# A 7x7 depthwise stage: work moved between ACT, DVE and GpSimd, and taps loaded a call ahead

## The chip, the cores and the metric

The kernel runs on one core of one Trainium2 chip. The metric is the device time of the program in microseconds. Three timed runs and one profiled execution of the kernel before are shown. A core has the engines PE (TensorE, matrix products), DVE (VectorE), ACT (ScalarE), POOL (GpSimd) and SP (which issues transfers). ACT and POOL issue transfers as well. Each engine runs its own instructions in a fixed order and waits on semaphores.

## The reference, cut to what matters

The program has four layers, each of the form x = x + layer(group norm(x)), on x of 4 batches, 384 channels and 64 x 64 pixels in float32. The change concerns the end of the third layer and the fourth.

The third layer ends with a mix that is linear in its second hidden tensor h2: per channel and batch, x2 = wx + gh * h2 + g0. The fourth layer is a depthwise 7 x 7 convolution whose kernel depends on the data:

```
x_w  = gelu(mean(x) @ w_avg.T + b_avg + max(x) @ w_max.T + b_max)
xr   = x_w[:, :, None, None] * w_mix          # 7 x 7 taps of each channel
Gx   = sqrt(sum(xr * xr));  Nx = Gx / (mean over channels of Gx + 1e-6)
kern = gamma * (xr * Nx) + beta
out  = depthwise_conv(x, kern, padding 3);    x = x + out
```

The kernel is therefore a factor of the channel and batch times the fixed taps `w_mix`, plus the constant `beta`. The program computes the two terms apart: a convolution with fixed taps, scaled afterwards, and a plain 7 x 7 box sum, scaled by beta.

## The kernel before, in words

The 384 channels lie in three tiles of 128 channels, j = 0, 1, 2. The stage is `phase_g`. In it:

- **x2.** `x2_of(j, b)` makes x2 for one tile and batch, 128 channels by 4096 pixels, in four quarters of 1024. A tile of wx is loaded into one of three `x` buffers, a quarter of h2 into one of three buffers with the tag `w7` (L1899, SP's queue). ACT scales two halves of it into PSUM (`x_m`, L1903), DVE adds them to x (L1906), ACT squares the sum for the variance (L1908, writing into the h buffer, which thereby becomes free after it), DVE takes the maximum (L1909). After four quarters POOL's queue stores x2 in DRAM (L1911).
- **Opening.** For j = 0 the four batches are made first, and `to_strips` lays each of them out for the convolution: POOL fills the edges (L1922, L1924), ACT scales (`ax`, L1925), PE transposes (L1935), ACT and DVE copy out of PSUM into `z` (L1942, L1940).
- **The fixed taps.** `conv7(j, c0)` convolves 8 channels of a tile, 16 calls for each tile, 48 in all. A call loads its taps (`wmix`, two buffers, L1950, SP's queue). Then, for each of four pairs of channels, an elementwise product of taps and a band mask builds a banded matrix (`toep`, four buffers, L1959), on POOL in every third pair and on DVE otherwise. DVE reads the band from PSUM, POOL from SBUF. PE multiplies it with `z` (eight matmuls of a pair, L1972). For j = 0 and 1 ACT copies the result out and stores it in DRAM (`raw`, L1981); for j = 2 DVE adds it to the rest of the output (L1984), which is stored.
- **The box sums.** `boxes(j, b)` takes a tile of x2 in four parts of 16 rows. POOL adds rows (L2021, L2023), DVE finishes the column of seven (L2024 to L2038). Then, for two halves of a part, PE transposes (`ht_m`, L2044), ACT copies out of PSUM (`ht`, L2046), PE multiplies with a band (`box_m`, L2050), and DVE scales and adds to x (L2052). For j = 0 and 1 `in_raw` is loaded and added (L2062). After four parts POOL's queue stores x (L2066, L2068).
- **Strips of later tiles.** `half_strips` loads x2 of the next tile from DRAM (L1858), ACT scales, PE transposes (L1868), ACT and DVE copy.
- **Factors.** After j = 0, `factors` derives the data-dependent scales from the means and maxima of x2; no box sum can be scaled before.

These functions are generators. The loop in `phase_g` takes them by turns: a call of `conv7` for 8 channels, then a piece of the strips, then up to five pieces of x2 (while j = 0) or of boxes (while j = 1 and 2). A scheduler fixes the order on each engine from the emitted program, with its own estimate of durations, so an instruction may stand earlier or later than it is emitted. It is these fixed orders, one for each engine, that run.

```
for n in range(8):
    self.conv7(j, 64 * half + 8 * n)
    next(strips, None)
    for k in range(5):
        if j == 0 and (k < 2 or k == 2 and n % 2):
            next(x2, None)
        if j == 1 or j == 2 and (k or n % 2):
            next(boxes, None)
```

Of the kernel before, what the change touches and what calls it, by code (L numbers as in the profile page):

```python
# [21 lines left out]
F32 = mybir.dt.float32  # L22
AF = mybir.ActivationFunctionType
ALU = mybir.AluOpType
# [4 lines left out]
NJ = 3  # L29
P = 128  # L30
# [251 lines left out]
class _Builder:  # L282
# [1403 lines left out]
    def phase_g(self):  # L1686

        tc, nc = self.tc, self.nc
        with ExitStack() as ctx:
            self.open_psum(ctx, 3)
            cp = ctx.enter_context(tc.tile_pool(name="g_const", bufs=1))
            self.gw_p = ctx.enter_context(tc.tile_pool(name="g_w", bufs=2))
            self.gt_p = ctx.enter_context(tc.tile_pool(name="g_t", bufs=2))
            self.w_gate = []  # L1700
            for j in range(NJ):
                t = cp.tile([P, 2, C], F32, tag=f"w_gate{j}", name="w_gate")
                for i, k in enumerate(("w_avg_t", "w_max_t")):
                    nc.scalar.dma_start(t[:, i], self.ins[k][:, j])
                self.w_gate.append(t)
            self.mean384 = self.const(cp, "mean384")
            self.band7 = self.const(cp, "band7")
            self.cols7 = self.const(cp, "cols7")

            self.band7_p = self.psum.tile([P, 512], F32, tag="band", name="band7_p", bufs=1)[:, 0:W]  # L1710
            nc.vector.tensor_copy(self.band7_p, self.band7)

            sq = self.gt_p.tile([P, 8 * 64], F32, tag="wmix", name="mix_sq")[:, 0 : NJ * 49]
            nc.vector.tensor_mul(sq, self.vec("w_mix"), self.vec("w_mix"))
            sq = sq.rearrange("p (j k) -> p j k", j=NJ)
            self.mix2 = cp.tile([P, NJ], F32, tag="mix2", name="mix2")
            nc.vector.tensor_reduce(self.mix2, sq, AX.X, ALU.add)
            self.ln_exp(nc.scalar.activation(self.mix2, self.mix2, AF.Sqrt))
            for k in ("a_s", "b_s"):
                setattr(self, k, cp.tile([P, NJ, B], F32, tag=k, name=k))  # L1720

            self.s_s, self.s_b = (cp.tile([P, NJ, B], F32, tag=k, name=k) for k in ("s_s", "s_b"))
            self.a_pair = cp.tile([P, NJ, 2, 2, 2], F32, tag="a_pair", name="a_pair")

            self.gm = cp.tile([P, NJ, B], F32, tag="gm", name="gm")
            self.off = cp.tile([P, NJ, B, 3], F32, tag="off", name="off")
            self.x2_var, self.x2_max = (cp.tile([P, NJ, B, 4], F32, tag=k, name=k) for k in ("x2_var", "x2_max"))


            self.z = self.z_[:, 0 : P * 136].rearrange("p (c k b) -> p c k b", k=34, b=B)  # L1730
            nc.gpsimd.memset(self.z_[:, P * 136 :], 0.0)
            nc.gpsimd.memset(self.z[:, :, 0], 0.0)
            self.group_means()
            behind = iter(())
            for b in range(B):
                for x in self.x2_of(0, b):
                    next(behind, None)
                for _ in behind:
                    pass
                behind = self.to_strips(0, b, x)  # L1740
            for _ in behind:
                pass
            self.pair_scales(1)

            def others(*pieces):
                for p in pieces:
                    yield from p

            x2 = others(*(self.x2_of(j, b) for j in (1, 2) for b in range(B)))
            boxes = others(*(self.boxes(j, b) for j, b in ((2, 0), (2, 1), (2, 2), (2, 3), (0, 0), (0, 1), (0, 2), (0, 3))))
            boxes1 = others(*(self.boxes(1, b) for b in range(B)))
            for j in range(NJ):
                for half in range(2):
                    strips = self.half_strips(j + half, 1 - half) if 0 < j + half < NJ else iter(())
                    for n in range(8):
                        self.conv7(j, 64 * half + 8 * n)
                        next(strips, None)
                        for k in range(5):  # L1760
                            if j == 0 and (k < 2 or k == 2 and n % 2):
                                next(x2, None)
                            if j == 1 or j == 2 and (k or n % 2):
                                next(boxes, None)
                    for _ in strips:
                        pass
                if j == 0:
                    for _ in x2:
                        pass
                    self.factors()  # L1770
                    self.pair_scales(2)
                if j == 1:
                    boxes = others(boxes, boxes1)
            for _ in boxes:
                pass
# [110 lines left out]
    def x2_of(self, j, b):  # L1886

        nc = self.nc
        at = lambda v: v[:, j, b : b + 1]
        if self.x2_ahead:  # L1890
            x = self.x2_ahead.pop(0)
        else:
            x = self.gx_tile("x2")
            nc.sync.dma_start(x, self.wx[b][:, j])
        for q in range(4):
            sl = slice(q * 1024, (q + 1) * 1024)

            h = self.gw_p.tile([P, 1024], F32, tag="w7", name="g_h2", bufs=3)
            nc.sync.dma_start(h, self.h2[b][:, j, sl])  # L1899
            for v in range(2):  # L1900
                m = self.pm("x2_m")
                part = slice(q * 1024 + v * 512, q * 1024 + v * 512 + 512)
                nc.scalar.activation(  # L1903
                    m, h[:, v * 512 : v * 512 + 512], AF.Identity, bias=at(self.g0), scale=at(self.gh)
                )
                nc.vector.tensor_add(x[:, part], x[:, part], m)  # L1906

            nc.scalar.activation(h, x[:, sl], AF.Square, bias=at(self.neg2), accum_out=self.x2_var[:, j, b, q : q + 1])  # L1908
            nc.vector.tensor_reduce(self.x2_max[:, j, b, q : q + 1], x[:, sl], AX.X, ALU.max)  # L1909
            yield None  # L1910
        nc.gpsimd.dma_start(self.scratch["x2"][b][j], x)  # L1911
        yield x

    def to_strips(self, j, b, x):
# [3 lines left out]
        for part in range(3):  # L1918
# [23 lines left out]
                    nc.scalar.copy(zv, mv.rearrange("p k c -> p c k"))  # L1942
            yield

    def conv7(self, j, c0):


        nc = self.nc
        wmix = self.gt_p.tile([P, 8 * 64], F32, tag="wmix", name="wmix")
        nc.sync.dma_start(wmix, self.ins["mix_t"][j][:, c0 : c0 + 8].rearrange("p c t n -> p (c t n)"))  # L1950
        o = self.gt_p.tile([P, 8, P], F32, tag="rest", name="rest_o", bufs=3)
        if j == NJ - 1:
            nc.sync.dma_start(o, self.rest[c0 : c0 + 8].rearrange("c y b n -> (y b) c n"))
        m = self.psum.tile([P, 1024], F32, tag="c", name="conv_m", bufs=2)
        for pair in range(4):
            t = self.gt_p.tile([P, 16, 8, 8], F32, tag="toep", name="toep", bufs=4)
            on_pool = (c0 // 2 + pair) % 3 == 2
            eng, band = (nc.gpsimd, self.band7) if on_pool else (nc.vector, self.band7_p)
            eng.tensor_tensor(  # L1959
                t,  # L1960
# [7 lines left out]
            for c in range(2):  # L1968
                ch = 2 * pair + c
                for i in range(4):  # L1970
# [5 lines left out]
                        start=i == 0,  # L1976
                        stop=i == 3,
                    )
        of = o.rearrange("p c n -> p (c n)")
        if j < NJ - 1:  # L1980
            nc.scalar.copy(of, m)  # L1981
            nc.scalar.dma_start(self.raw[j][:, c0 : c0 + 8], o)
            return
        nc.vector.tensor_add(of, of, m)  # L1984
        nc.sync.dma_start(self.out[j][:, c0 : c0 + 8], o)

    def boxes(self, j, b):

# [2 lines left out]
        nc = self.nc  # L1991
        x = self.load_x2(j, b)
        off = lambda k: self.off[:, j, b, k - 6 : k - 5]
        scale = self.b_s[:, j, b : b + 1]
        pairs_of = lambda t, r, n: t[:, r * W : (r + 2 * n) * W].rearrange("p (k r w) -> p k r w", r=2, w=W)
        above, last = None, None
        for part in range(4):
# [42 lines left out]
            for q in range(2):  # L2040
# [3 lines left out]
                    nc.tensor.transpose(m[:, k * P : (k + 1) * P], h[:, at : at + P], self.ident)  # L2044
                ht = self.gt_p.tile([P, 512], F32, tag="ht", name="ht")
                nc.scalar.copy(ht, m)  # L2046
                m = self.pm("box_m")
                for k in range(4):
                    sl = slice(k * P, (k + 1) * P)
                    nc.tensor.matmul(m[:, sl], lhsT=ht[:, sl], rhs=self.cols7, start=True, stop=True)  # L2050
                xq = x[:, (2 * part + q) * 512 : (2 * part + q + 1) * 512]
                nc.vector.scalar_tensor_tensor(xq, m, scale, xq, ALU.mult, ALU.add)  # L2052
                if q == 0:
                    yield
            if j < NJ - 1:
                d = self.gt_p.tile([P, 1024], F32, tag="rest", name="in_raw", bufs=3)
                nc.sync.dma_start(
# [5 lines left out]
            if part == 3:  # L2063
# [2 lines left out]
                    nc.gpsimd.dma_start(self.out[j].rearrange("(b m) c n -> b (m c n)", b=B)[b].rearrange("(c n) -> c n", c=P), x)  # L2066
                else:
                    nc.gpsimd.dma_start(self.rest[:, :, b], x.rearrange("p (y n) -> p y n", n=P))  # L2068
            yield


@with_exitstack
# [29 lines left out]
```

## Time and profile before

| | us |
|---|---|
| median of three runs | 4841.11 (4838.23 to 4847.09) |
| the profiled execution | 4841.52 |
| its span | 4839.6 |
| start of the stage `phase_g`, from the span's start | about 4075 |
| first product of `conv7` | 4163.5 |
| first DVE operation of `factors` with x2's variance | 4354.9 |
| last matmul | 4834 |

Over the whole span PE is busy 91%, DVE 60%, ACT 41% and POOL 16%; the stage of this document is the last 765 us of it. In that stage the sums are: PE 599, DVE 611, ACT 335 and POOL 315 us.

How to read the lines of the profile that follow: a line of the groups gives the line of the code, the engine, the operation, output and inputs, their shapes and the count, then the busy time in us and the mean of one in ns, and after the next bar how long the engine stood idle just before these instructions, and what ended that idle time. A line of the waits gives who waited, for whom, the total in us, the number of times and the longest. A transfer's profile interval is its issue, not its transfer. Matmul records are two for each float32 matmul in the code and one for each transpose; they overlap, so their durations don't add up to time.

### The profile page before, as it was taken

The numbers are of one execution on the slowest core, as the hardware profiler recorded it, in microseconds if no ns is written. First come the engines' busy times: TensorE is split into PE (matmuls) and PEld (weight loads), VectorE is DVE, ScalarE is ACT, GpSimd is POOL, SyncE is SP. The second block draws the span as 40 slices with busy tenths as digits, with TensorE's granted clock in tenths as the row PEclk, the third lists the DMA queues.
The fourth block names the chain that finished last, engine by engine and source line by source line (L and its number), as shares of the span: only waits on it lengthen the run. The fifth ranks groups of instructions, "written<-read, shape, count | busy, mean of one in ns | idle before, by whom it ended". The sixth has DMA issues, their size and how long they took to land.

```text
span 4839.6 us, 49747 instructions
## 1 busy us (share of the span) xinstructions
PE 4399.5 (91%) x18445; PEld 2453.7 (51%) x18445; DVE 2892.0 (60%) x4647; ACT 1996.9 (41%) x2976; POOL 757.7 (16%) x643
## 2 busy tenths in 40 slices
PE   6999999999999999989987898699999997778888
PEld 2233444344443444435477787344444443678888
DVE  7766556645656455556867777555521113767898
ACT  4444444444444444336345566211133334763321
POOL 1000000000000000000044554000000001235544
PEclk9999999999999999989988999899999998788999
DMA  4312212111211111113168898776664444995776
GB/s 145 102 42 66 72 53 75 64 56 42 70 61 63 40 59 59 53 63 120 65 197 282 278 308 299 273 259 251 238 236 153 156 156 152 325 346 183 231 256 232
DMA packets 289663, 747.65 MB, mean 154 GB/s; under 512 B 22555, under 2 KB 123014, under 8 KB 277382
## 3 DMA queue, kind: packets, MB, share of 16 engines
q1 hardware_dynamic: 226744, 454.62, 29.4%
q0 software_dynamic: 36480, 167.01, 9.2%
q10 hardware_dynamic: 26190, 122.76, 6.4%
q8 instruction: 149, 2.44, 0.2%
q14 instruction: 100, 0.82, 0.1%
HBM read 442.04 MB, written 302.25 MB: 154 GB/s over the span
## 4 chain that ended last, share of the span: by engine, by line
PE 32%; DVE 7%; DMA 6%; ACT 3%; issue 2%; POOL 1%; SPq 0%; ACTq 0%; DVEq 0%; POOLq 0%
PE h_m L1658 10%; PE h_s L1604 10%; PE conv_m L1370 6%; PE conv_m L1972 2%; DMA c_d<-d 2%; DMA wmix<-in_mix_t 1%; DMA g_h<-h 1%; DVE toep L1959 1%; PE box_m L2050 1%; DVE in_x L2052 1%; DMA ax<-x 1%; DVE in_x L2062 1%; DMA unit_x<-x 1%; DVE box L2034 0%; ACT g_h L1908 0%
## 5 line engine op out<-in xcount | busy, mean ns | idle before, releaser
L819 ACT ACTIVATE probs<-sc_s 128x1024 f32<-128x1024 f32 x512 | 496.5, 1019 | 695.0 <-PE av L929 594.8
L929 PE MATMUL av<-probs,vt 128*128 128x512 f32 x1536 | 717.7, 604 | 0.0
L1128 DVE SCALAR_TENSOR_TENSOR acc<-band,vecs,acc 128x512 f32<-128x512 f32 x708 | 496.0, 745 | 44.9 <-POOL band L1089 39.6
L1658 PE MATMUL h_m<-f_h,cm_w_t 128*128 128x512 f32 x1152 | 497.3, 595 | 7.4 <-ACT f_h L1646 7.4
L1370 PE MATMUL conv_m<-toep,z 128*128 128x192 f32 (+1 forms) x2304 | 444.2, 354 | 9.5 <-DVE z L1299 9.4
L929 PEld LDWEIGHTS av<-probs,vt 128*128 128x128 f32 x1536 | 277.6, 192 | 339.6 <-issue 335.9
L1972 PE MATMUL conv_m<-toep,z 128*128 128x128 f32 x3072 | 395.5, 287 | 36.5 <-POOL toep L1959 15.8
L1370 PEld LDWEIGHTS conv_m<-toep,z 128*128 128x128 f32 x2304 | 408.5, 197 | 31.6 <-DVE z L1299 10.1
L1972 PEld LDWEIGHTS conv_m<-toep,z 128*128 128x128 f32 x3072 | 381.1, 203 | 38.4 <-POOL toep L1959 16.2
L1604 PE MATMUL h_s<-e_tok,cm_w_t 128*128 128x512 f32 x768 | 362.9, 595 | 4.2 <-DVE e_tok L1589 4.2
L1658 PEld LDWEIGHTS h_m<-f_h,cm_w_t 128*128 128x128 f32 x1152 | 220.4, 191 | 284.4 <-issue 273.3
L1666 DVE BATCH_NORM_STATS2 h_st<-f_h 128x6 f32<-128x512 f32 x96 | 66.5, 694 | 429.8 <-ACT f_h L1665 429.8
L811 PE MATMUL sc_s<-q,k 32*128 32x512 f32 x2048 | 307.1, 643 | 15.1 <-ACT probs L819 14.9
L1351 POOL TENSOR_TENSOR toep<-w,band 128x1280 f32<-128x1280 f32 x94 | 272.6, 2900 | 237.5 <-PE conv_m L1370 234.3
L1051 PE MATMUL t_m<-w_in_t,xb 128*128 128x384 f32 x768 | 282.0, 503 | 3.4 <-DVE coef L1068 3.2
L965 PE MATMUL proj_m<-xm,w_proj_t 128*128 128x512 f32 x576 | 270.3, 609 | 6.4 <-DVE xm L904 4.9
L1611 ACT COPY e_h<-h_s 128x1024 f32<-128x1024 f32 x96 | 97.2, 1012 | 400.2 <-PE h_s L1604 400.2
L1613 DVE BATCH_NORM_STATS2 h_st<-e_h 128x6 f32<-128x512 f32 x192 | 123.4, 685 | 204.9 <-ACT e_h L1611 204.7
L1604 PEld LDWEIGHTS h_s<-e_tok,cm_w_t 128*128 128x128 f32 x768 | 146.9, 191 | 187.9 <-issue 183.1
L1051 PEld LDWEIGHTS t_m<-w_in_t,xb 128*128 128x128 f32 x768 | 144.4, 194 | 141.6 <-issue 62.5
L972 DVE SCALAR_TENSOR_TENSOR x_res<-proj_m,bn_c,x_res 128x512 f32<-128x512 f32 x96 | 71.7, 747 | 240.2 <-PE proj_m L965 240.2
L1604 PE MATMUL h_s<-z,cm_w_t 128*128 128x512 f32 x384 | 196.7, 594 | 0.0
(423 smaller groups left out, 6396.3 us busy)
## 6 DMA issues: line engine op xcount, KB each, us to landing
d<-d_o ACTq DMA_DIRECT2D x48, 1024.0 KB
c_d<-d SPq DMA_DIRECT2D x48, 1024.0 KB
hid<-e_h ACTq DMA_DIRECT2D x16, 3072.0 KB
f_h<-hid SPq DMA_DIRECT2D x16, 3072.0 KB
x_in<-in_x SPq DMA_DIRECT2D x96, 256.0 KB
x_res<-in_x SPq DMA_DIRECT2D x32, 768.0 KB
xa<-x_res POOLq DMA_DIRECT2D x32, 768.0 KB, 3.9
xa_out<-xa SPq DMA_DIRECT2D x32, 768.0 KB
```

What stands on the lines that cost most here:

```text
L811: nc.tensor.matmul(s[:, g], lhsT=k4[32 * g : 32 * g + 32, c], rhs=q[i][32 * g : 32 * g + 32], start=True, stop=True,)
L819: nc.scalar.activation(p[:, h * 1024 : (h + 1) * 1024], s[:, 2 * h : 2 * h + 2].rearrange("p a b -> p (a b)"), AF.Exp, scale=0.25,)
L929: nc.tensor.matmul(av[0], lhsT=vt[:, 4 * c + v, :], rhs=p[:, v * 512 : (v + 1) * 512], start=c == 0 and v == 0, stop=c == 7 and v == 3,)
L965: nc.tensor.matmul(m, lhsT=self.w_proj[:, j, o * P : (o + 1) * P], rhs=xm[:, j], start=j == 0, stop=j == NJ - 1,)
L1051: nc.tensor.matmul(m[:, 0:C], lhsT=xb[:, j], rhs=self.w_in[:, j, :], start=j == 0, stop=j == NJ - 1,)
L1128: nc.vector.scalar_tensor_tensor(out, src(j, k), w, done, ALU.mult, ALU.add)
L1351: eng.tensor_tensor(t, self.w53[:, at : at + 160].rearrange("p (m n) -> p m n", n=8).unsqueeze(2).to_broadcast([P, 20, 8, 8]), band.rearra ...
L1370: nc.tensor.matmul(m[:, c * 256 + to : c * 256 + to + 64 * (k1 - k0)], lhsT=self.z_[:, at : at + P], rhs=t[:, 10 * c + k0 : 10 * c + k1].r ...
L1604: nc.tensor.matmul(s[:, v, :], lhsT=w1[:, j, o * P : (o + 1) * P], rhs=t[j][:, v * 512 : (v + 1) * 512], start=j == 0, stop=j == NJ - 1,)
L1613: nc.vector.bn_stats(st[:, o, 8 * b + 2 * i + v, :], h[:, o, v * 512 : (v + 1) * 512])
L1658: nc.tensor.matmul(m, lhsT=w2[:, o, j * P : (j + 1) * P], rhs=h[:, o, v * 512 : (v + 1) * 512], start=o == 0, stop=o == 5,)
L1972: nc.tensor.matmul(m[:, ch * P : (ch + 1) * P], lhsT=self.z_[:, at : at + P], rhs=t[:, 8 * c + 2 * i : 8 * c + 2 * i + 2].rearrange("p m a ...
```

## The change

Four edits, all in the last stage:

1. In `x2_of`, for j = 0 alone, the product gh * h2 + g0 runs on POOL over the whole quarter, in place in the h buffer, and one DVE add of 1024 columns takes it from SBUF. For j = 1 and 2 ACT and PSUM are used as before.
2. The taps are loaded by a new function `load_mix`, on POOL's queue, at the start of the call before the one that uses them; the first is loaded ahead of the loop.
3. `conv7` becomes a generator that yields after each pair and at its end, so that the pieces of x2 or boxes come between pairs. For j = 1 and 2 every second pair's product is on POOL, for j = 0 every third as before.
4. In `boxes`, the matmul with the band and the add that follows move into `box_sums` and are emitted one piece later than the transposes and the copy that feed them.

```diff
+            self.load_mix(0)
...
-                        self.conv7(j, 64 * half + 8 * n)
-                        next(strips, None)
-                        for k in range(5):
+                        for k, _ in enumerate(self.conv7(j, 64 * half + 8 * n)):
+                            if k == 0:
+                                next(strips, None)
...
-            for v in range(2):
-                m = self.pm("x2_m")
-                part = slice(q * 1024 + v * 512, q * 1024 + v * 512 + 512)
-                nc.scalar.activation(
-                    m, h[:, v * 512 : v * 512 + 512], AF.Identity, bias=at(self.g0), scale=at(self.gh)
-                )
-                nc.vector.tensor_add(x[:, part], x[:, part], m)
+            if j == 0:
+                nc.gpsimd.tensor_scalar(h, h, at(self.gh), at(self.g0), ALU.mult, ALU.add)
+                nc.vector.tensor_add(x[:, sl], x[:, sl], h)
+            else:
...
+    def load_mix(self, n):
+        if n < 16 * NJ:
+            c0 = n % 16 * 8
+            self.mix_ahead = self.gt_p.tile([P, 8 * 64], F32, tag="wmix", name="wmix")
+            src = self.ins["mix_t"][n // 16][:, c0 : c0 + 8]
+            self.nc.gpsimd.dma_start(self.mix_ahead, src.rearrange("p c t n -> p (c t n)"))
...
-        wmix = self.gt_p.tile([P, 8 * 64], F32, tag="wmix", name="wmix")
-        nc.sync.dma_start(wmix, self.ins["mix_t"][j][:, c0 : c0 + 8].rearrange("p c t n -> p (c t n)"))
+        wmix = self.mix_ahead
+        self.load_mix(16 * j + c0 // 8 + 1)
...
-            on_pool = (c0 // 2 + pair) % 3 == 2
+            on_pool = pair % 2 == 1 if j else (c0 // 2 + pair) % 3 == 2
...
+            yield
         of = o.rearrange("p c n -> p (c n)")
...
-                m = self.pm("box_m")
-                for k in range(4):
-                    sl = slice(k * P, (k + 1) * P)
-                    nc.tensor.matmul(m[:, sl], lhsT=ht[:, sl], rhs=self.cols7, start=True, stop=True)
-                xq = x[:, (2 * part + q) * 512 : (2 * part + q + 1) * 512]
-                nc.vector.scalar_tensor_tensor(xq, m, scale, xq, ALU.mult, ALU.add)
                 if q == 0:
                     yield
+                    self.box_sums(j, b, x, 2 * part, ht)
+            yield
+            self.box_sums(j, b, x, 2 * part + 1, ht)
...
+    def box_sums(self, j, b, x, n, ht):
+
+        nc = self.nc
+        m = self.pm("box_m")
+        for k in range(4):
+            sl = slice(k * P, (k + 1) * P)
+            nc.tensor.matmul(m[:, sl], lhsT=ht[:, sl], rhs=self.cols7, start=True, stop=True)
+        xq = x[:, n * 512 : (n + 1) * 512]
+        nc.vector.scalar_tensor_tensor(xq, m, self.b_s[:, j, b : b + 1], xq, ALU.mult, ALU.add)
```

## The prediction

> **What bounds the kernel now.** The change touches only the last stage, `phase_g`, so I read the stretches of that stage first, then the groups by line, then who waited for whom. The stretches (us from the span's start; length; busy time of PE, its weight loads, DVE, ACT, POOL; clock; DMA share; GB/s) are the opening (first channel tile), the 7x7 products of j = 0, and two halves of the rest:
>
> ```profile
> 4075.00:4163.00 88.00, 34.92 (x134) 23.35 (x134) 59.04 (x83) 80.64 (x105) 10.69 (x22) 0.52 0.86 307
> 4163.00:4361.00 198.00, 155.25 (x1218) 152.72 (x1219) 136.28 (x157) 118.31 (x171) 64.24 (x39) 0.88 0.95 340
> 4361.00:4600.00 239.00, 205.73 (x1660) 199.39 (x1659) 197.87 (x239) 87.36 (x159) 131.25 (x96) 0.94 0.66 200
> 4600.00:4840.00 240.00, 203.56 (x1659) 198.22 (x1657) 218.21 (x220) 48.27 (x98) 108.82 (x66) 0.94 0.74 246
> ```
>
> Three different limits. In the opening ACT is busy 80.6 of 88 us. From 4163 to 4361 no engine is near full, but the DMA engines are at 0.95 and 340 GB/s: this stretch waits for bytes. From 4361 on DVE (197.87 + 218.21 = 416.1 of 479 us) and PE (409.3) share the limit, POOL is half idle (240.1), ACT nearly free.
>
> The groups by line in that stage (count, busy us, mean ns, idle before):
>
> ```profile
> L1903 ACT ACTIVATE x_m<-g_h,g,gh 128x512 f32<-128x512 f32 x96 | 71.3, 774 | 52.8 <-DMA g_h<-h 44.2 <-DVE x L1906 7.6 <-DVE z L1873 1.0
> L1959 DVE TENSOR_TENSOR toep<-wmix,band_p 128x1024 f32<-128x1024 f32 x129 | 155.4, 1211 | 28.0 <-DMA wmix<-in_mix_t 18.5 <-PE conv_m L1972 7.5 <-issue 1.6
> L1959 POOL TENSOR_TENSOR toep<-wmix,band 128x1024 f32<-128x1024 f32 x63 | 152.2, 2417 | 176.7 <-PE conv_m L1972 105.4 <-DMA wmix<-in_mix_t 62.6 <-issue 5.9
> L2024 DVE TENSOR_TENSOR box<-box,box 128x512 f32<-128x512 f32 x48 | 51.6, 1084 | 13.2 <-POOL box L2023 13.2
> L2029 DVE SCALAR_TENSOR_TENSOR box<-edge,off,box 128x128 f32<-128x128 f32 x36 | 32.7, 907 | 0.4 <-PE ht_m L2044 0.4
> ```
>
> A product of taps and band (`toep`) takes DVE 1.21 us and POOL 2.42 us. L2029 needs 907 ns for 128 columns where L2024 needs 1084 for 512: part of these times is not work. The lines' own views give the reason (minimum/median/maximum):
>
> ```profile
> L2024 DVE TENSOR_TENSOR box<-box,box x48: 660/690/2882, 4367.2 to 4803.2; 128x512 f32<-128x512 f32 x48
> L2029 DVE SCALAR_TENSOR_TENSOR box<-edge,off,box x36: 317/344/4112, 4374.9 to 4804.9; 128x128 f32<-128x128 f32 x36
> ```
>
> and the timeline shows one of them:
>
> ```profile
> 4682.68 2.34 POOL L1959 TENSOR_TENSOR toep<-wmix,band 128x1024 f32<-128x1024 f32 x1
> 4682.69 2.88 DVE L2024 TENSOR_TENSOR box<-box,box 128x512 f32<-128x512 f32 x1
> ```
>
> The DVE add began 0.01 us after a POOL product, stood until it ended, then ran its 0.6 us. Mean less median, times count, is the time lost so: L2024 18.5, L2030 10.9, L2034 13.6, L2029 20.3, L2062 11.3 and L2027 5.4 us, 80 us together. So DVE is 416 us busy, of which only 336 are work. Last, the waits inside the second half (4361 on, whose two halves I add):
>
> ```profile
> PE box_m L2050 <- ACT ht L2046: 21.3, 12, 5.4
> DVE in_x L2052 <- PE box_m L2050: 14.5, 11, 4.3
> DVE box L2024 <- POOL box L2023: 11.2, 13, 3.1
> ...
> PE box_m L2050 <- ACT ht L2046: 17.1, 11, 4.1
> DVE in_x L2052 <- PE box_m L2050: 8.0, 7, 3.7
> ```
>
> PE stands 38.4 us for the copy of the transposed box, and DVE 22.5 us for the sums that follow.
>
> **What the skill says.** The Trainium skill, "SBUF — State Buffer", section "Who interferes with whom": a DVE instruction with two SBUF inputs contends with a GpSimd instruction that reads SBUF, as an exclusive lock; one with at most one SBUF input does not. The trace agrees: the pair above, and L1959 on DVE, whose band lies in PSUM, stays at 1202 to 1225 ns. "GPSIMD Engine Reference", section 4.1: two-input elementwise work is about 2x slower there than on VectorE, one-input roughly at line rate. The first is seen here (2417/1211 = 2.0); no run here shows the second at this size. "DMA: Bandwidth & Descriptors", Specifications: some 358 GB/s of HBM for a core. Agreed: windows of this stage reach 354 and 358 GB/s at 0.97 to 0.98 of DMA share.
>
> **Part 1: gate product of the first tile on GpSimd.** Removed: 32 ACT operations of 0.774 us (24.8 us of ACT's 80.6) and 32 DVE adds of 0.683 (21.9). Added: 16 adds of 128x1024 with both inputs in SBUF on DVE, 1.22 us each (L850 has this form: 1218 ns), 19.5 us, and 16 products on POOL. That product isn't in the trace. From below: POOL's 128x128 `tensor_scalar` (L1103) takes 0.597 us, and 896 more columns at the line rate that the same page gives in section 3.1 (1.03 cycles an element, 1.2 GHz: 0.86 ns) give 1.37 us. From above: all of L1103 scaled by eight is 4.8 us. POOL's two-input slope, (2332 - 1258)/512 = 2.1 ns a column, would make 2.5. I take 1.9: 30 us in the opening, between 22 and 77. DVE's adds now meet the lock; say 0.6 us each, 10 us. ACT then needs 80.6 - 24.8 = 56, DVE 59 - 21.9 + 19.5 + 10 = 67, POOL 41 of the 88 us. No engine binds, so the bytes do: three transfers of 2.1 MB per batch (x, h2, x2 store), 6.3 MB at 345 GB/s = 18.3 us, against (4160 - 4083)/4 = 19.3 us now (first gate product and last strip in the timeline). And what the opening prefetches less, the next stretch must fetch. From 4075 to 4361 the DMA engines idle 0.14 x 88 + 0.05 x 198 = 22 us; a shorter opening recovers about a third: **-8 us**, between -18 and +10 (POOL at 4.8 us is the late one then). Queued behind the new product on POOL: the x2 stores and zero fills, which already wait for DVE and PE there; a product of the next batch waits behind the store of the last, about one add (1.2 us) a batch, inside the sum.
>
> **Part 2: taps loaded a call ahead on POOL's queue.** All 48 loads leave SP and cost POOL 0.585 us each (L1337 has the like), 32 of them after 4361: 19 us of its idle 239. The wait for the two `wmix` buffers moves too: on POOL's queue the next products stand behind it, but it waits for products of the call before, already done. The DVE's wait for taps (18.5 us) lies wholly before 4361, where bytes bind anyway, and x2 stores of 2 MB (12.9 us to landing there) now precede the taps on the same queue: 0 there. After 4361 SP no longer stops for it: **-1 us** (the wait on `in_raw` is 2.2 us). If the cover goes, a call late by 5 us in every fourth of 32 costs 40; I hold that unlikely because a call lasts 15 us there.
>
> **Part 3: every second product on POOL for j = 1, 2.** POOL has 21 of 64 per tile now and gets 32: 22 move. DVE loses 22 x 1.21 = 26.6 us, POOL gains 22 x 2.36 = 51.9, and reaches 240 + 52 + 19 = 311 of 479 us. But the lock grows. A DVE operation that arrives at random waits in proportion to the sum of squared POOL durations: 42 x 2.36² + 96 x 1.38² = 417 now, 64 x 2.36² + 183 = 539 then, so 80 us becomes 103.5, +23.5 (ends: 0, and +51.9 if each moved product holds DVE for its whole length). **Net -3 us**, between -27 and +25.
>
> **Part 4: pair by pair, box sums one piece later.** No operation is added. In the changed order on PE the matmuls between a box's transposes and its sums rise from a median of 4 to 8 (two records each; the chain of waits has 40 such records in 4.47 us, 0.112 apiece: 0.9 to 1.8 us), with 16 of 96 left at 4; the ACT copy between them takes 0.58 us. PE's 38.4 us of waiting should mostly go. What this gives the end is what DVE, the other bound, waited: three quarters of 22.5, **-17 us**, between 0 and -25.
>
> Sum: -8 - 1 - 3 - 17 = -29. The profiled execution took 4841.5 us (span 4839.6 and 1.9 around it), the median of the runs is 4841.1, so one basis: 4841.5 - 29 = 4812.5, say 4812.
>
> **Rivals.** (a) Slower: the lock. The interleaving sets POOL products beside DVE's box work, with DVE's own lock-free products spread out. If each moved product holds DVE 2.36 us, part 3 is +25, DVE is late again and part 4 gives nothing; with the opening at -4 the time is 4862. It decides when the lock costs over 26.6/22 + 9/22 = 1.6 us per moved product, against my 23.5/22 = 1.07. For it: the 80 us already lost. Against: DVE stops standing once POOL is past, and box work is unchanged in amount. (b) No change: bytes hide part 1 wholly, parts 3 and 4 refill each other: 4836. For it: 340 GB/s before 4361. (c) Better: the lock grows by 10 only, waits go entirely, opening -12: 4841.5 - 12 - 17 - 25 = 4788. For it: PE's work after 4361 is some 371 us (3316 records at 0.112) of 479.
>
> **Chances.** Forecast (4795 to 4831) 0.42, (c) 0.18, (b) 0.20, (a) 0.20. Within 0.2% is about what a measurement of this kernel can't tell from no change. Faster 0.42 + 0.18 = 0.60, same 0.20, slower 0.20. The range leaves out the far ends of (a) and (c): 4776 to 4862.
>
> **What would show it.** Right: 16 POOL products near 1.9 us; opening plus j = 0 near 278 us at 0.95 DMA share; DVE still near 413 us busy after 4361, with L2024's successor near 1.2 us mean; PE's wait on `ht` below 15 us; DVE's wait on the sums below 8. Wrong: a POOL product above 4 us, the successor of L2024 above 1.6 us, or PE waiting for POOL's `toep` by tens of us.

## The result, and the profile after

The change made the kernel slower: 4864.48 us (median of seven runs, 4859.18 to 4872.72) against 4841.11 us (seven runs), a ratio of 1.005 with a 95% interval of 1.0038 to 1.0062, or 23 us. The forecast was 4812 us. The range, 4776 to 4862, ended 2 us below the result. The profiled execution of the kernel after has a span of 4861.8 us.

The stage has to be cut at the same events in both kernels, since its start wanders by some 10 us from one execution to the next with work that the change doesn't touch. I cut at the last matmul ahead of the stage, the first matmul of `conv7`, the first DVE operation of `factors` on x2's variance, and the end. The stretches of the kernel before and then after, with the columns of the prediction's first table:

```profile
4068.90:4163.50 94.60, 35.50 (x137) 23.39 (x135) 63.50 (x109) 82.22 (x109) 11.38 (x24) 0.54 0.82 292
4163.50:4354.87 191.37, 149.62 (x1174) 147.28 (x1175) 132.55 (x146) 115.11 (x167) 58.72 (x36) 0.87 0.95 338
4354.87:4839.60 484.73, 414.89 (x3360) 403.02 (x3358) 419.35 (x470) 138.34 (x260) 245.59 (x166) 0.94 0.71 226
```

```profile
4066.80:4166.00 99.20, 32.76 (x137) 26.94 (x135) 62.49 (x91) 62.61 (x76) 38.67 (x43) 0.52 0.75 271
4166.00:4353.76 187.76, 147.03 (x1146) 144.06 (x1147) 131.70 (x144) 114.49 (x166) 68.78 (x52) 0.88 0.98 346
4353.76:4861.80 508.04, 423.19 (x3388) 411.18 (x3387) 421.01 (x450) 139.54 (x262) 319.85 (x217) 0.92 0.67 217
```

Opening and j = 0 together took 287.0 us against 286.0: ACT's 20 us less in the opening bought nothing. Nearly all of the loss is in the last stretch, 508.0 against 484.7. (Not quite all: the cut is an event on DVE, and 28 matmul records that lay ahead of it now lie behind it, 1146 and 3388 against 1174 and 3360. At 423.19/3388 = 0.125 us each that is some 3.5 us of PE's work that only changed sides; the opening itself is 4.6 us longer.) In the last stretch DVE is as busy as before (421.0 against 419.4), although 22 products have left it. PE is busy 8 us longer, these 3.5 among them, at a granted clock of 0.92 against 0.94, and its idle time (length less busy) grew from 69.8 to 84.9 us.

The groups by line of the kernel after, with the same columns as before, and the two lines' own views (minimum/median/maximum ns):

```profile
L1971 POOL TENSOR_TENSOR toep<-wmix,band 128x1024 f32<-128x1024 f32 x85 | 204.5, 2407 | 104.9 <-PE conv_m L1984 72.5 <-DMA wmix<-in_mix_t 29.7 <-issue 2.6
...
L1971 DVE TENSOR_TENSOR toep<-wmix,band_p 128x1024 f32<-128x1024 f32 x107 | 129.0, 1211 | 14.4 <-PE conv_m L1984 6.4 <-DMA wmix<-in_mix_t 5.9 <-issue 1.9
...
L2037 DVE TENSOR_TENSOR box<-box,box 128x512 f32<-128x512 f32 x48 | 58.0, 1211 | 20.6 <-POOL box L2036 20.5
...
L2042 DVE SCALAR_TENSOR_TENSOR box<-edge,off,box 128x128 f32<-128x128 f32 x36 | 37.0, 1027 | 0.9 <-PE ht_m L2057 0.7
...
L1902 POOL TENSOR_SCALAR g_h<-g_h,gh,g 128x1024 f32<-128x1024 f32 x16 | 25.9, 1621 | 25.1 <-DMA g_h<-h 25.0
```

```profile
L2037 DVE TENSOR_TENSOR box<-box,box x48: 671/692/2827, 4363.0 to 4811.0; 128x512 f32<-128x512 f32 x48
L2042 DVE SCALAR_TENSOR_TENSOR box<-edge,off,box x36: 332/700/3965, 4377.6 to 4821.9; 128x128 f32<-128x128 f32 x36
```

L2037 is the successor of L2024, and its mean rose from 1084 to 1211 ns at an unchanged median (690, 692): more of its instances are held. L2042 (L2029 before) is now held in half of its instances: the median went from 344 to 700 ns. The waits of the last stretch:

```profile
PE box_m L2086 <- ACT ht L2059: 47.6, 20, 5.2
PE ht_m L2057 <- DVE in_x L2088: 11.1, 9, 3.3
...
DVE in_x L2088 <- PE box_m L2086: 33.6, 22, 9.1
DVE box L2037 <- POOL box L2036: 20.5, 17, 6.1
```

All of them grew (38.4, 0.9, 22.6 and 13.2 us before), though the box sums now stand a piece later. One place of the timeline shows how the wait on `ht` comes about (start, length, engine and line, and in brackets the idle time before it):

```profile
4649.71 0.60 PE L2057 MATMUL ht_m<-ident,box 128*128 128x128 f32 x4
...
4650.21 2.35 POOL L1971 TENSOR_TENSOR toep<-wmix,band 128x1024 f32<-128x1024 f32 x1
4650.28 2.83 DVE L2037 TENSOR_TENSOR box<-box,box 128x512 f32<-128x512 f32 x1 [0.79 <-POOL box L2036]
...
4653.20 0.30 ACT L2029 COPY box<-box 128x128 f32<-128x128 f32 x1 [5.71 <-DVE box L2037]
...
4653.40 0.58 ACT L2059 COPY ht<-ht_m 128x512 f32<-128x512 f32 x1
...
4654.03 1.80 PE L2086 MATMUL box_m<-cols,ht 128*128 128x128 f32 x8 [1.94 <-ACT ht L2059]
```

The transposes were ready at 4650.3. But a POOL product began 0.07 us ahead of DVE's add L2037 and held it 2.1 us. In ACT's fixed order another copy (L2029, the rows carried to the next part) stands ahead of the `ht` copy, and it waited for this add. So ACT, idle for 5.7 us, could not copy `ht` until the hold was over, and PE waited 1.94 us, although this `ht` doesn't depend on the add.

### The profile page after: what moved, and what is told of

It reads as the page before. It is cut to its first block, busy times and chain, and to the rows that moved or that the text cites. A ratio compares the mean times of both kernels' runs of the same rounds, so it can differ in the third digit from the quotient of the medians.

```text
span 4861.8 us, 49676 instructions
## 1 busy us (share of the span) xinstructions
PE 4400.0 (91%) x18445; PEld 2457.4 (51%) x18445; DVE 2892.1 (59%) x4609; ACT 1978.4 (41%) x2944; POOL 868.9 (18%) x729
## 3 DMA queue, kind: packets, MB, share of 16 engines
q8 instruction: 149, 2.44, 0.2%
## 5 line engine op out<-in xcount | busy, mean ns | idle before, releaser
L1971 POOL TENSOR_TENSOR toep<-wmix,band 128x1024 f32<-128x1024 f32 x85 | 204.5, 2407 | 104.9 <-PE conv_m L1984 72.5
```

Of the source, the lines that this page charges most:

```text
L1971: eng.tensor_tensor(t, wmix[:, pair * 128 : pair * 128 + 128] .rearrange("p (m n) -> p m n", n=8) .unsqueeze(2) .to_broadcast([P, 16, 8, 8 ...
```

## The experiments

Two theories are tested. The **lock theory**: a POOL product that reads SBUF holds DVE's operations with two SBUF inputs, and DVE's box work is late. The **order theory**: the holding matters little; each engine's order is fixed, and POOL's long products delay the POOL box adds behind them, then DVE, ACT and PE in turn. All times below are medians with the ratio to the kernel before, run beside them. "DVE held" is, for all DVE groups of the last stretch, busy time less count times the mean duration of the same group in `e12_none_and_pairs`, where little is held (so it is 0 there by construction). The last three columns are of the last stretch of one profiled execution of each kernel, and how much they scatter was not measured. Some of these executions lie well off their kernel's median: e5's by 19 us, e6's by 12 and e3's by 10 above it, e4's by 8 below.

| kernel | us | ratio (95%) | DVE held | DVE busy | PE waits for `ht` |
|---|---|---|---|---|---|
| before | 4841.1 | 1 | 71 | 419 | 38 |
| after | 4864.5 | 1.0050 (1.0038 to 1.0062) | 95 | 421 | 48 |
| e1 part 1 | 4839.8 | 0.9998 (0.9987 to 1.0009) | 70 | 418 | 35 |
| e2 part 2 | 4839.9 | 0.9992 (0.9982 to 1.0001) | 68 | 417 | 42 |
| e3 part 3 | 4855.7 | 1.0030 (1.0020 to 1.0040) | 75 | 401 | 51 |
| e4 part 4 | 4837.0 | 0.9989 (0.9977 to 1.0001) | 56 | 401 | 44 |
| e8 parts 3, 4 | 4853.5 | 1.0031 (1.0020 to 1.0042) | 83 | 406 | 41 |
| e5 after, third on POOL | 4844.5 | 1.0016 (1.0006 to 1.0027) | 62 | 412 | 42 |
| e6 after, quarter on POOL | 4834.5 | 0.9983 (0.9973 to 0.9993) | 49 | 410 | 36 |
| e7 after, none on POOL | 4822.3 | 0.9959 (0.9940 to 0.9978) | 1 | 398 | 22 |
| e9 e7 + idle product | 4873.1 | 1.0062 (1.0040 to 1.0083) | 82 | 477 | 39 |
| e10 e7 + idle fill | 4832.6 | 0.9987 (0.9971 to 1.0003) | 33 | 416 | 27 |
| e11 before, none on POOL | 4823.3 | 0.9969 (0.9957 to 0.9982) | 12 | 406 | 32 |
| e12 part 4, none on POOL | 4809.6 | 0.9938 (0.9920 to 0.9956) | 0 | 394 | 16 |

**The four parts alone.** Each is the kernel before with one part of the diff of the change.

Part 1 (`x2_of` for j = 0 on POOL):

> The kernel before with part 1 alone (the first tile's gate product on GpSimd). Lock theory (the loss comes from POOL work that holds DVE after 4361): part 1 is neutral, within 4 us of before, 4837 to 4845. Order theory (edits make waits queue up behind each other on POOL, ACT and PE): the changed kernel's opening, from the last hidden matmul to the first 7x7 matmul, took 99.7 us against 95.1, so part 1 alone costs 3 to 8 us: 4844 to 4849. The prediction's own step said 8 us faster: 4833.

Part 2 (`load_mix`, a call ahead, on POOL's queue):

> The kernel before with part 2 alone (taps loaded a call ahead on POOL's queue). Lock theory: 4838 to 4843, nothing moves. Order theory: the loads put waits for DVE into POOL's fixed order ahead of the products, so 5 to 12 us slower: 4846 to 4853.

Part 3:

```diff
-            on_pool = (c0 // 2 + pair) % 3 == 2
+            on_pool = pair % 2 == 1 if j else (c0 // 2 + pair) % 3 == 2
```

> The kernel before with part 3 alone (every second product on POOL for the last two tiles). Lock theory: this carries the loss, 15 to 25 us slower, 4856 to 4866, with the box groups on DVE 30 us or more above their medians times counts than before. Order theory: DVE loses 26 us of work and the lock gives 10 to 15 back, so 4830 to 4842.

Part 4 (yields between pairs, `box_sums` a piece later):

> The kernel before with part 4 alone (products pair by pair with pieces between, box sums one piece later). Lock theory: PE waits less for the box copy, 4825 to 4838. Order theory: the pieces stand in another order on ACT and PE, and the copy of the transposed box queues behind copies that wait for DVE or a transfer: 10 to 20 us slower, 4851 to 4861.

Measured: parts 1 and 2 make no difference that can be told; neither does part 4 (some 5 us, with an interval that just reaches 1), and PE waits no less for `ht` with it (44 us against 38), though the lock theory had expected it to; part 3 costs some 15 us (1.003). So part 3 loses, but not quite as the lock theory had it: the time is at the lower end of what it expected, and the 30 us of growth in the box groups did not appear (75 us held against 71 in all).

That total hides a growth. I put each DVE operation that ran more than 0.06 us over its group's median in `e12_none_and_pairs` down to the POOL instruction that it overlapped longest. The excess beside POOL's products is then 54.6 us before and 54 to 60 us in the six other kernels with 42 products (e1, e2, e4, e5, e13, e14), but 71.9 us in e3 and 68, 69, 73 and 80 us in the others with 64 (e15, e17, e8, after); with 32 (e6) it is 39.8. What shrank in e3 is the excess beside POOL's own box adds, from 28.0 to 13.9 us. So part 3 alone does add some 17 us of lock.

Still DVE lost 19 us of busy time, lock included, and the kernel got slower. The stretch of this kernel:

```profile
4365.53:4864.20 498.67, 414.72 (x3360) 402.01 (x3358) 400.53 (x449) 138.91 (x260) 299.92 (x186) 0.94 0.69 219
```

Set beside `e4_pairs_and_shift`, with 401.30 us of DVE and 19 us less of this stretch (480.1 us), this says that DVE's busy time doesn't set the end.

**The amount on POOL.** Three kernels differ from the kernel after only in the share of products that POOL makes for j = 1 and 2:

```diff
-            on_pool = pair % 2 == 1 if j else (c0 // 2 + pair) % 3 == 2
+            on_pool = (c0 // 2 + pair) % 3 == 2                             # e5
+            on_pool = pair == 3 if j else (c0 // 2 + pair) % 3 == 2         # e6
+            on_pool = not j and (c0 // 2 + pair) % 3 == 2                   # e7
```

> Parts 1, 2 and 4 of the change, POOL's share of the products left at a third as before. Both theories blame the bigger POOL share, so both expect the loss to go: 4830 to 4838 us, about the sum of what parts 1, 2 and 4 gave alone (4841.9 - 2.2 - 2.1 - 4.9 = 4832.7). Above 4848 the loss lies in a combination of parts 1, 2 and 4, and both fall.

> The whole change, but for j = 1 and 2 every fourth product on POOL (16 of 64 per tile, the last pair of each call) in place of every second. Lock theory: against a third, DVE takes 10 products more (+12 us) and the lock shrinks by 80 x 56/417 = 10.7 us, so within 3 us of the run with a third, 4830 to 4840. Order theory (POOL's products delay what stands behind them on POOL, and with it DVE's column sums, ACT's copies and PE): 5 us faster than with a third.

> The whole change, but for j = 1 and 2 no product on POOL at all; DVE makes all 64 of a tile. Lock theory: against a third, 42 products more on DVE (+51 us), lock smaller by 80 x 234/417 = 45 us; time 4836 to 4846, and the time follows DVE's busy time. Order theory: no long POOL instruction stands ahead of a box add any more, PE's wait for the ht copy falls from about 44 to under 25 us, time 4815 to 4828. If DVE's work alone decides (no lock gain), DVE becomes the limit and it is slower than 4860.

With 64, 42, 32 and 0 products on POOL the times are 4864, 4844, 4834 and 4822 us, and the held time is 95, 62, 49 and 1 us. On average each product taken off POOL gave 42/64 = 0.66 us, though it put 1.21 us of work on DVE; the steps are uneven (10 us for the 10 products from a third to a quarter, 12 us for the next 32). A quarter came out within the lock theory's numbers, but not within 3 us of the run with a third, as that theory had it; none came out below them (4836 to 4846 expected). The theory let relief and lock cancel, and so counted DVE's work at full value. The order theory's numbers for e7 came out, but its reason is not yet shown. The run with a third missed both theories (1.0016 where 4830 to 4838 was expected); see the last group.

**Lock or order.** Parts 3 and 4 together, without 1 and 2:

> Parts 3 and 4 of the change without parts 1 and 2. Alone they gave +13.7 and -4.9 us. If they add up: 4851. If the interleaving makes the bigger POOL share worse (box pieces now emitted between the products): 4858 to 4868, the whole loss of the change. Lock theory expects the first and box groups longer by 15 us; order theory expects the second, with PE's waits for the ht copy and for the sums over 55 us together.

They give 1.0031, against 1.0030 for part 3 alone, so its loss isn't made worse by the interleaving. The deciding pair starts from e7 and gives POOL's time back, once with reads of SBUF and once without. Both write a `toep` buffer that nobody reads, in every second pair of j = 1 and 2:

```diff
+            if j and pair % 2 == 1:
+                u = self.gt_p.tile([P, 16, 8, 8], F32, tag="toep", name="extra", bufs=4)
+                nc.gpsimd.tensor_tensor(u, taps, self.band7, ALU.mult)          # e9 (operands as L1971)
...
+                nc.gpsimd.memset(u, 0.0)                                        # e10
+                nc.gpsimd.memset(u, 0.0)
+                nc.gpsimd.memset(u[:, 0:10], 0.0)
```

> The change with no POOL product for j = 1 and 2 (4822 us), but POOL makes an extra product of taps and band in every second pair of these tiles, as the change does, into a toep buffer that nobody reads; DVE still makes all 64 products of a tile. It puts back POOL's work (64 x 2.4 = 154 us) without taking any from DVE. Lock theory: the lock comes back (12 us to some 95 us) on top of DVE's full work of 385 us, so DVE needs 480 of the 478 us of the rest: 4860 to 4900 us. Order theory: POOL's long instructions delay the box adds: also slower, 4840 to 4865, with DVE's wait on POOL's box adds at 20 us.

> As the run with the extra product, but in its place POOL fills the same buffer with zeros three times (128x1024, 128x1024, 128x640; about 2.4 us together), which occupies POOL and its order as long and takes the same buffers, but reads nothing from SBUF. Nothing of the computation changes. Lock theory: no lock without reads, so DVE's two-input operations stay at their unblocked times and the time stays within 8 us of 4822. Order theory: the same delay as with the product, 4840 to 4865.

Groups of e9 and of e10 in the last stretch, and the first fill of e10 that meets the add:

```profile
L1982 POOL TENSOR_TENSOR extra<-wmix,band 128x1024 f32<-128x1024 f32 x63 | 153.5, 2437 | 43.2 <-PE conv_m L1995 40.0 <-DVE in_x L2099 2.7
...
L2048 DVE TENSOR_TENSOR box<-box,box 128x512 f32<-128x512 f32 x48 | 55.9, 1175 | 1.7 <-POOL box L2047 1.7
```

```profile
L1982 POOL MEMSET extra<- 128x1024 f32 x63 | 60.5, 961 | 39.8 <-PE conv_m L1989 39.4
L1983 POOL MEMSET extra<- 128x1024 f32 x63 | 60.2, 956 | 1.4
L1984 POOL MEMSET extra<- 128x640 f32 x63 | 40.3, 640 | 1.0
...
L2042 DVE TENSOR_TENSOR box<-box,box 128x512 f32<-128x512 f32 x48 | 34.6, 725 | 8.2 <-POOL box L2041 8.1
```

```profile
4362.75 0.94 POOL L1982 MEMSET extra<- 128x1024 f32 x1 [4.38 <-PE conv_m L1989]
...
4363.16 0.68 DVE L2042 TENSOR_TENSOR box<-box,box 128x512 f32<-128x512 f32 x1
```

POOL is busy for the same time (315 and 317 us in the stretch), but with the product DVE's add needs 1175 ns and the kernel 4873 us, with the fill 725 ns and 4833. An add that starts in the middle of a fill runs its 0.68 us. DVE's wait for POOL's box adds, which the order theory put at 20 us, is 1.7 us with the product. The product costs 1.0062 - 0.9959 = 0.0103, some 50 us; the fill 0.0028, some 13 us, with intervals that overlap, a little over the 8 us that the lock theory allowed. So in this kernel, where DVE makes every product itself, roughly three quarters of what POOL's extra products cost is the lock, and up to a quarter is POOL's time and order (and the buffer that both take). One difference between the two runs is not the lock: the product also reads the taps and so keeps their buffer from the next load. But the waits of these loads for it come to only 3.2 us in e9.

In e10 some 33 us are still held. Of the 48 DVE operations that ran more than 0.06 us over their median there, 42 overlapped one of POOL's box adds, which read SBUF. The others show a second thing, which neither theory had: the fills held one kind of operation too, L2045, where DVE adds a scalar to a tile of SBUF. It has a single tile as input, and alone it takes 0.28 us.

```profile
L2045 DVE TENSOR_SCALAR box<-box,off x12: 277/1184/3696, 4366.5 to 4772.3; 128x128 f32<-128x128 f32 x12
```

```profile
4735.08 0.95 POOL L1983 MEMSET extra<- 128x1024 f32 x1
4735.50 0.61 DVE L2045 TENSOR_SCALAR box<-box,off 128x128 f32<-128x128 f32 x1
```

Each of the eight L2045 that met a fill ended 0.08 to 0.09 us after a fill ended. Some 12 of the 33 us are on this line, so the fill is not quite free of holding, and the lock's share above is if anything too low.

**Without POOL's products.** The kernel before, and before with part 4, with `on_pool = not j and (c0 // 2 + pair) % 3 == 2`:

> The kernel before with no POOL product for j = 1 and 2, nothing else changed: DVE makes all 64 of a tile. If POOL's share is the only lever: 4841 - 17 = 4822 to 4826 us, as with the whole change. If the interleaving and the shifted sums (part 4) are what makes room for it: 4830 to 4840.

> Part 4 of the change and no POOL product for j = 1 and 2; parts 1 and 2 left out. Lock theory: with the lock gone, PE's wait for the box chain is what is left, and part 4 gives what was forecast for it, 4810 to 4822 us, at or below the run that also has parts 1 and 2 (4822).

Their waits, e11 and then e12:

```profile
PE box_m L2050 <- ACT ht L2046: 31.7, 19, 6.5
...
DVE in_x L2052 <- PE box_m L2050: 30.1, 24, 7.0
```

```profile
PE box_m L2074 <- ACT ht L2047: 16.3, 11, 3.8
...
DVE in_x L2076 <- PE box_m L2074: 26.9, 11, 7.5
```

Taking 42 products off POOL alone gives 0.9969, 15 us faster. Adding part 4 then gives another 0.0031, again 15 us, where with POOL's products in place part 4 gave 0.0011, which can't be told from nothing. Part 4 is worth about the 17 us of the forecast, but only once no product holds the chain: then PE's wait on `ht` falls to 16 us. Which of its two edits does it, the yields between pairs or the later sums, was not tried apart. The move of the products has a price as well: PE now waits for DVE's `toep`, 3.1 us in e11 and 14.6 us in e12, where it had not waited before.

**Part 2 in company.** Parts 1, 2 and 4 gave 1.0016 together and nothing bad alone. Four combinations of the parts as the change's diff has them (2 and 4; 1 and 4; all but 2; 1 and 4 with no product on POOL):

> Parts 2 and 4 of the change, without 1 and 3. If the taps' loads on POOL's queue are what costs 13 us beside part 4 (a load stands on that queue for DVE's product of the call before, and the box adds behind it): 4844 to 4850, as with parts 1, 2 and 4 (4844.5). If they cost nothing and part 1 does: 4834 to 4838.

> Parts 1 and 4 of the change, without 2 and 3. If the taps' queue is the cause: 4833 to 4838, the sum of the two alone. If part 1 is, by the order of the opening: 4844 to 4850.

> The whole change without part 2, the taps loaded on SP's queue in their own call as before. If the taps' queue is the cause: 4850 to 4856 (after's 4864.5 less some 11 us). If part 1 or the combination of 1 and 3 is: 4860 to 4867.

> Parts 1 and 4 and no POOL product for j = 1 and 2, taps on SP's queue as before. If the taps' queue is the cause: 4805 to 4813, as without parts 1 and 2 (4809.6). If part 1 is: 4820 to 4826.

Measured: parts 2 and 4, 4844.1 (1.0003, 0.9992 to 1.0014); parts 1 and 4, 4831.9 (0.9983, 0.9974 to 0.9992); the whole change without part 2, 4848.8 (1.0015, 1.0005 to 1.0025); none on POOL with parts 1 and 4, 4815.0 (0.9941, 0.9927 to 0.9956). Three of the four lie 1 to 2 us outside what was expected if the taps are the cause, but each is nearer to that than to the other case. So it is part 2, not part 1: in the whole change it costs 1.0050 - 1.0015 = 0.0035, some 17 us, with three such pairs pointing the same way (e5 less e14 0.0033, e13 less e4 0.0014, e7 less e16 0.0018; the intervals of the last two pairs overlap).

```diff
-            self.nc.gpsimd.dma_start(self.mix_ahead, src.rearrange("p c t n -> p (c t n)"))
+            self.nc.sync.dma_start(self.mix_ahead, src.rearrange("p c t n -> p (c t n)"))
```

> The whole change, but the taps' loads, still a call ahead, are issued on SP's queue. If POOL's queue is what costs (0.58 us of POOL for each load and its place before the box adds): 4844 to 4852, as without part 2 (4848.8). If the earlier place of the load is what costs, whatever the queue: 4860 to 4866.

> The same with no POOL product for j = 1 and 2. If POOL's queue is what costs: 4806 to 4815, as with parts 1 and 4 alone (4815.0, ratio 0.9941) or a little better, since a load ahead spares DVE its waits for taps. If the earlier place costs: 4820 to 4826, as with the taps on POOL's queue (4822.3, ratio 0.9959).

(The diff is that of e17 against the kernel after; e18 also has no product on POOL.) These two disagree. In the whole change the load on SP's queue keeps the loss (4860.7, ratio 1.0042, 1.0028 to 1.0056), which blames the earlier place; with no POOL product it removes it (4808.6, 0.9938, 0.9926 to 0.9951), which blames POOL's queue. That part 2 costs in company is shown; by which of its two edits, and how, stays open.

e12 and e18 are the fastest kernels found, some 30 us faster than before; they can't be told apart.

## Why the prediction was wrong

The four terms were -8, -1, -3 and -17 us. Measured alone they are about 0, 0, +15 and -5, and part 2 in company is +17. The mechanism failed in parts 3 and 4, the size in part 1, and for part 2 a term was missing.

**Part 1 (-8).** The duration of the product was close: mean 1.62 us where 1.9 was taken, though its median of 1.20 lies under the 1.37 that was to be the bound from below. Its worth was not close. ACT's busy time in the opening fell from 82.2 to 62.6 us, but alone the part gave 0.9998. The opening and j = 0 in that kernel took 92.9 + 193.1 = 286.0 us, exactly as before, with 0.96 of DMA share in the second stretch: what the opening saves, the stretch that waits for bytes takes back. Rival (b) had said so for this part. (The bytes don't go at one rate, either: in pieces of 20 us of this stretch of the kernel before, at a DMA share of 0.97 to 1.01, they went at 296 to 392 GB/s, so that the 358 of the prediction is no ceiling of a piece.) With the taps on POOL's queue as well, the opening took 99 to 100 us in each of the six kernels that have both (92.5 and 95.2 with them on SP's queue); why is not settled.

**Part 2 (-1).** Alone right (0.9992, no difference). In the whole change it costs some 17 us, and I had no term for a combination. DVE's wait for taps, on which my "if the cover goes" rested, is not how: after 4361 it doesn't appear among DVE's waits. Set beside e15, which lacks part 2, the kernel after is 6.6 us longer in the opening, 2.7 shorter in j = 0 and 17.6 longer in the last stretch, where 80 us in place of 68 are held beside POOL's products. So the place is known, in one execution of each, but not how the earlier loads bring it about.

**Part 3 (-3), the step that failed.** Its balance of DVE was right for the whole change: 26.6 us of products leave, the lock adds 24 (95 less 71; beside POOL's products alone 25) where 23.5 was forecast, and DVE's busy time in the stretch is 421.0 against 419.4. That it came so close is luck in part: in the four other kernels with 64 products the growth beside them is 13 to 18 us. Wrong was to call this balance a time. The two sides are not worth the same. The products that left stand ahead of PE in four `toep` buffers, read their band from PSUM and are not held (1.20 to 1.23 us each in the kernel before); nobody waited for them (`toep` is not among PE's waits in this stretch of the kernel before). The held operations are mostly the column sums, on the chain POOL, DVE, ACT, PE that ends in the wait on `ht`. That e11 makes 42 products more on DVE and is 15 us faster is the same statement from the other side. "DVE and PE share the limit" was therefore a misreading: DVE's 416 us included some 70 to 80 of being held, as the prediction had itself found, and taking work from it gave nothing. Two of its signs of being right came true (DVE near 413 us, the successor of L2024 near 1.2 us) and the kernel lost: they watched DVE, not the chain.

**Part 4 (-17).** The step "PE's 38.4 us of waiting should mostly go" failed: 47.6 us in the kernel after, 43.6 with the part alone. I counted the matmuls between transposes and sums and the 0.58 us of the copy, but not what stands ahead of that copy in ACT's order. Where a carried row copy stands there and waits for a held add, a distance of a few microseconds doesn't help. With no product to hold it, the term was nearly right in size: e11 to e12, 15 us. But the way to it was not the one forecast: the 17 were three quarters of DVE's wait for the sums, which hardly fell (30.1 to 26.9 us), while PE's wait on `ht` fell by 15.4. That the sizes agree is luck.

**The rivals.** Rival (a), "Slower: the lock", came within 3 us of the result. Its place and kind of loss were right, its point of decision was not: it asked for 1.6 us held per moved product, and the kernel lost with 24/22 = 1.1, my own figure, because the relief that it set against the hold was worth nothing. The nearness of its number is luck: it took each moved product to hold DVE for 2.36 us, twice what was measured, and 17 of the 23 us belong to part 2, which it didn't name.

The Trainium skill's sentence in "SBUF — State Buffer", "Who interferes with whom", that DVE's two-input instructions contend with a GpSimd instruction that reads SBUF and not with one that only writes it, held in the run made for it: the add L2042 of e10 has a mean of 725 ns beside fills, where it is 1175 beside products, and the 14 adds that met nothing but fills took 0.69 us at most. L2045 shows that this is no rule for every DVE instruction: it has one input in SBUF, and both products and fills held it. Its "Perfetto Trace Analysis", section "Optimizing Scalar/DVE Operations", warns that moving work between GpSimd and DVE may not help, because they share a port; the measured form of this is the row of four shares above.

One thing is left open on part 3 alone. In e3 PE is busy as long as before (414.7 against 414.9 us in the last stretch), so its loss is all idle time (84.0 against 69.8), and the wait on `ht` grew by 13 us. Some 17 us more are held there beside POOL's products; whether that is the whole cause, or POOL's order did its part, was not tried on this kernel. The pair that separates the two, e9 and e10, stands on another one.

## What to carry to other kernels

A microsecond saved on a busy engine and a microsecond lost on it are equal only if both lie on the path that somebody waits for: before moving work off an engine, look whether anyone waits for that work, and what the moved work will hold. When mean and median of a group are far apart, count the excess as waiting, not as load, and try the opposite move too (here: all products back on the "full" engine). A longer distance between producer and consumer helps only if nothing in the queue between them is late for another reason.

## What the runs showed of the hardware

- A product on POOL with both inputs in SBUF held DVE's 128x512 add for its rest (2.83 us in place of 0.69), and a fill on POOL did not (0.68 us, begun inside one). A fill of 128x1024 f32 takes POOL 0.96 us.
- DVE's add of a scalar to a 128x128 f32 tile, which has one input in SBUF, was held by both: 0.28 us alone, up to 2.44 us beside POOL's products (L2040 of the kernel after), 0.61 us in the fill shown above.
- 42 products on POOL held DVE for 54 to 60 us in seven kernels, 64 for 68 to 80 us in five: 1.1 to 1.4 us for each product of 2.4 us.
- POOL's product with two scalars per channel, 128x1024 f32 with one tensor input, takes 1.20 us (median), half of its product of two tensors (2.41 us, a mean), and about as long as DVE's product of two tensors (1.21 us).
- The granted clock of PE in the last stretch was 0.92 after and 0.94 before, with 8 us more of PE busy time, of which 3.5 are work from the other side of the cut; `e14_gate_and_pairs` had 0.91 with 423 us busy and was faster than before, so no conclusion is drawn from it.
